# Transposes of q's and k's inputs, the squares of their angles, and the router's first rows moved to other places in one attention chunk's order

## The chip, the cores and the metric

The kernel runs on one NeuronCore of one Trainium2 chip. A core has five engines that run side by side, each with its own queue of instructions: TensorE (PE in the profile; its weight loads are PEld), VectorE (DVE), ScalarE (ACT), GpSimd (POOL) and SyncE (SP, which issues most DMA transfers here). Engines wait for each other through semaphores. The metric is the device time of one execution in microseconds (us). Before the change the median of three runs is 3440.44 us (3437.03 to 3441.25).

## What is computed

One pre-norm transformer block on x of shape (8, 1024, 512), in float32. Attention first, then a mixture of experts, each with its residual:

```python
theta_q = xh / (1.0 + jnp.abs(w_q)) + b_q + t * phi_q      # the same for k
sin_q, cos_q = lookup_sin_cos(theta_q)                     # table of 2048, linear interpolation
Q = jnp.concatenate([cos_q, sin_q], axis=-1)
V = cos_v + sin_v
scores = jnp.where(causal, -jnp.inf, jnp.einsum('bqhd,bkhd->bhqk', Q, K) / scale)
out = jnp.einsum('bhqk,bkhd->bqhd', jax.nn.softmax(scores, axis=-1), V).reshape(B, S, D)
theta_out = out / (1.0 + jnp.abs(w_out)) + b_out
...
x = x + attn(_layernorm(x))                                # 16 heads of 32
x = x + ffn(_layernorm(x))                                 # 8 experts, the best 2 of each token, 160 places each
```

The router of the experts takes a softmax over 8 logits of each token, keeps the best two, and numbers the tokens of each expert in order. The experts are two matrix products with a ReLU between.

## The kernel before

**Chunks.** Attention runs over 32 chunks, n = 0 to 31: batch b = n // 4, and c = n % 4 for the four heads (128 columns) that a chunk holds. A chunk has two pairs of heads. Each pair takes ten score tiles (`scores`, L591): matrix products into a PSUM tile of two banks, then one exponential on ScalarE (L620). `attend` (L626) multiplies the exponentials with v. `turn` (L658) transposes a pair's result back to tokens and divides by the sums. All score tiles, all transposes of `turn` and `qk_pre`, and all small products of the router take their PSUM tile from one pool, `ps_sc`, of three tiles in rotation: a new tile waits until the last reader of the tile three places before it is done.

**Sines.** For the next chunk's q and k, `qk_pre` (L479) transposes the normalized input (L202) and makes integer angles p on VectorE (L495, four instructions); `angle` (L425) shifts them left into r. ScalarE then takes two absolutes of r into c (L506), two squares of p's low half, in place (L430), and the sines of c and r (L514, L433). `qk_post` (L517) multiplies c and r with the squares on VectorE (L436) and sends each to the pairs' tiles with four transfers on SyncE's queue (L527). The pool `qkt` holds one buffer each of p, r and c: the shift into r for chunk n+2 may write only when the four transfers of r for chunk n+1 have read it. Sine and exponential are in different table sets of ScalarE, so that a chunk has two table loads; squares and absolutes need none. v (`v_pre`, `v_post`) and the attention's output (`o_pre`, `o_post`) go through the same steps: shift, sine, square, product.

**Residual and router.** `o_post` (L569) adds the output of chunk n-1 to x_mid (L575) and takes layernorm statistics of it (L577, eight instructions). When a batch's four chunks are in, `router` (L687) runs in steps that other code advances with `next(route)`: statistics to a mean and an inverse root, and the first two rows normalized (L704, by twos) and sent to DRAM (L710); then, four times, a feature step (L202 transposes of two rows, the copies L731 from PSUM to xT, the next two rows) and a sum step (L748 and L765 on TensorE, L770 and L772 on VectorE); then the choice of experts. Feature step g and sum step g belong together: L765 multiplies the xT that L731 wrote. `load_mid` (L370) loads the next batch's x into x_mid, on SyncE's queue, once the last two rows have been made from the old one.

**Order.** For TensorE, ScalarE and VectorE the order of instructions is the order in which the program emits them. The loop at L1202 writes it out with generators: `some(k, ...)` advances by k tiles, `rest` to the end. In the first half of chunk n (pair 0) it emits the last seven attend tiles of chunk n-1, in two pieces, each followed by five score tiles; `with_asides` sets small VectorE work between tiles. Then come `turn` of chunk n-1's second pair, `o_pre`, ten attend tiles of pair 0, the sines, and the first VectorE product of the next chunk. The second half (pair 1) emits two score tiles, `turn`, three score tiles, three attend tiles, five score tiles. Around these the code before has

```python
        if more:
            next_pairs = rest(post)
            v_post(n + 1, v_st)
        some(3, *ahead)
        router_step()
        if late:
            square(o_st[0])
            o_post(n - 1, o_st)
        some(3, attend(n, 1, 0, es[0], halves1))
        router_step()
        if late and c == 0:
            route = router(b - 1)
            next(route)
        some(5, *ahead)
        if n + 2 < NCK:
            qk_st = rest(qk_pre(n + 2))
            angle(*qk_st)
        if late and c == 0:
            next(route)
```

`late` is true from the second chunk on, `more` until the last but one, and `route` exists from n = 4 on. After the loop the expert half follows (L1134); the last batch's router runs in it (`ending`, L1331).

Of the kernel before, what the change touches and what calls it, by code (L numbers as in the profile page):

```python
# [73 lines left out]
def preln_attn_moe_kernel(  # L74
# [21 lines left out]
    nc = tc.nc  # L96
# [328 lines left out]
    def angle(p, r):  # L425
        nc.vector.tensor_scalar(r, p, TURN_SHIFT, None, ALU.logical_shift_left)

    def square(p):
        f = p.bitcast(U16).rearrange("p (s two) -> p s two", two=2)[:, :, 0]
        nc.scalar.activation(p.bitcast(F32), f, AF.Square, bias=split_c, scale=1.0 / FINE)  # L430

    def sine(r):
        nc.scalar.activation(r.bitcast(F32), r, AF.Sin, scale=STEP_ACT)  # L433
# [67 lines left out]
    def qk_abs(st):  # L501

        f, r = st
        c = qkt.tile([P, 2, S], F32, name="qk_c")
        for i in range(2):
            nc.scalar.activation(c[:, i, :], r[:, i, :], AF.Abs)  # L506
            yield c, f, r
        for i in range(2):
            square(f[:, i, :])
            yield c, f, r  # L510

    def qk_sin(st):
# [17 lines left out]
    def by_token(t):  # L530
        return t.rearrange("p (t f) -> p t f", f=P)
# [25 lines left out]
    def v_post(n, st):  # L557
        times(v_tiles[n % 2][:, :, :, :DH], heads(st[0]), heads(st[1].bitcast(F32)))


    def o_pre(n, pos):
        c = n % NCH
        p = pos.bitcast(I32)
        r = trig.tile([P, S], I32, name="t_r")
        nc.vector.tensor_tensor(by_token(p), by_token(pos), along(bias_o, c), ALU.add)
        angle(p, r)
        return p, r

    def o_post(n, st):  # L569
        f, s = st[0], st[1].bitcast(F32)  # L570
        b, ch = divmod(n, NCH)
        times(s, f, s)
        xt, stats = mid_tiles[b]
        xs = xt[:, :, ch * P : (ch + 1) * P]
        nc.vector.scalar_tensor_tensor(xs, by_token(s), SUM_UNIT, xs, ALU.mult, ALU.add)  # L575
        for t in range(NTT):
            nc.vector.bn_stats(stats[:, t, ch, :], xt[:, t, ch * P : (ch + 1) * P])  # L577

# [47 lines left out]
    def attend(n, pr, h, es, halves):  # L626

        vt = v_tiles[n % 2]
        av = ps_av.tile([P, 512], F32, name="av")
        tiles = tiles_of(h)  # L630
        for i, parts in enumerate(tiles):
            for kb, q0, w, at in parts:
                for a in range(2):
                    nc.tensor.matmul(  # L634
                        av[a * 64 : (a + 1) * 64, q0 - 512 * h :],
                        lhsT=vt[:, kb, 2 * pr + a, :], rhs=es[i][:, a, at : at + w],
                        start=kb == 0, stop=i + 1 == len(tiles),
                    )
            if i + 1 == len(tiles):
                av_sb = avp.tile([P, 512], F32, name="av_sb")  # L640
                q = 2 * (n % NCH) + pr
                nc.vector.tensor_scalar(av_sb, av, inv_o[:, q : q + 1], None, ALU.mult)
                halves.append(av_sb)
            yield

    def some(count, *gens):

        for gen in gens:
            while count and next(gen, 0) is None:
                count -= 1  # L650

    def rest(gen):
        got = None
        for got in gen:
            pass
        return got
# [214 lines left out]
    def keep(box, gen):  # L871
        for box[0] in gen:
            yield
# [311 lines left out]
    rest(base1)  # L1185
    mask()
    v_st = rest(v_pre(0))
    cs = qk_abs(qk_st)
    next(cs)
    qk_st = next(cs)  # L1190
    nc.scalar.activation(qk_st[0], qk_st[0], AF.Sin, bias=quarter_c, scale=-STEP_ACT)
    rest(cs)
    sine(qk_st[2])
    pairs = rest(qk_post(qk_st))
    sine(v_st[1])
    square(v_st[0])
# [2 lines left out]
    load_base(1)  # L1199
    last = None  # L1200
    o_st = route = first_rows = None
    for n in range(NCK):  # L1202
        more, late = n + 1 < NCK, last is not None
        b, c = divmod(n, NCH)
        if n == NCK - 1:
            to_inputs.close()
            first_rows = experts_begin()
        pos_n = trig.tile([P, S], F32, name="o_p")
        if late:
            e11, halves1, pos = last  # L1210
        es, halves = [[], []], [[], []]

        products = [attend(n, 0, h, es[h], halves[0]) for h in range(2)]
        if late:
            products.insert(0, attend(n - 1, 1, 1, e11, halves1))
        ahead = [scores(pairs[0], h, es[h]) for h in range(2)]
        places, v_box = [None], [None]
        absolutes = keep(places, qk_abs(qk_st)) if more else iter(())  # L1220
        asides = [keep(v_box, v_pre(n + 1))] if more else [first_rows]
        if b == 0 and c in (1, 2):
            asides.append(layernorm1(1, c - 1))
        elif c == 0 and b + 1 < B:
            asides.append(layernorm1(b + 1, 1))
        elif c == 3 and b + 2 < B:
            asides.append(layernorm1(b + 2, 0))

        router_step = lambda: next(route) if c == 1 and route is not None else None

        def with_asides(count):
            for _ in range(count):
                some(1, *ahead)
                for g in asides:
                    next(g, None)

        if late:
            some(3, *products)
        router_step()
        if c == 2 and route is not None:  # L1240
            next(route)
            asides.append(part(route))
        if n == 0:
            with_asides(3)
            qk_st = rest(qk_pre(1))
            angle(*qk_st)
            absolutes = keep(places, qk_abs(qk_st))
            with_asides(2)
        else:
            with_asides(5)  # L1250
        router_step()
        some(2, absolutes)
        if late:
            some(4, *products)
        router_step()
        with_asides(5)
        router_step()
        rest(absolutes)
        for g in asides:
            rest(g)  # L1260
        if more:
            v_st = v_box[0]
            square(v_st[0])
        if n == 1:
            load_mid(0)
        if late:
            turn(1, halves1, pos)
            o_st = o_pre(n - 1, pos)
        if c == 1 and b > 0:
            load_mid(b)  # L1270
        if n == 2:
            load_b1()
        if c == 2 and b + 2 < B:
            load_x(b + 2)
        if c == 3 and b > 0:
            next(route)
            if b > 1:
                fetch_slots(b - 2)
            scatter()


        some(3, *products)
        if more:
            qk_st = places[0]
            qk_sin(qk_st)
            sine(v_st[1])
        if late:
            sine(o_st[1])
        if more:
            post = qk_post(qk_st)  # L1290
            next(post)
        some(NTT, *products)
        if n == 0:
            load_base(2)


        es, halves1 = [[], []], []
        ahead = [scores(pairs[1], h, es[h]) for h in range(2)]
        router_step()
        if c == 2 and route is not None:  # L1300
            next(route)
        some(2, *ahead)
        turn(0, halves[0], pos_n)
        if more:
            next_pairs = rest(post)
            v_post(n + 1, v_st)
        some(3, *ahead)
        router_step()
        if late:
            square(o_st[0])  # L1310
            o_post(n - 1, o_st)
        some(3, attend(n, 1, 0, es[0], halves1))
        router_step()
        if late and c == 0:
            route = router(b - 1)
            next(route)
        some(5, *ahead)
        if n + 2 < NCK:
            qk_st = rest(qk_pre(n + 2))
            angle(*qk_st)  # L1320
        if late and c == 0:
            next(route)
        if n + 3 < NCK:
            load_base(n + 3)
        last = (es[1], halves1, pos_n)
        pairs = next_pairs if more else None
    rest(attend(NCK - 1, 1, 1, es[1], halves1))
    turn(1, halves1, pos_n)
    to_pairs.close()
# [1 line left out]
    def ending():  # L1331

        o_st = o_pre(NCK - 1, pos_n)
        yield
        sine(o_st[1])
        square(o_st[0])
        for _ in range(3):
            yield
        o_post(NCK - 1, o_st)
        for _ in range(3):  # L1340
            yield
        for name in router(B - 1):

            for _ in range(5 if name == "tiles" else 1):
                yield
        fetch_slots(B - 2)
        scatter()
        fetch_slots(B - 1)
# [33 lines left out]
```

## Time and profile before

| | us |
|---|---|
| median of three runs | 3440.44 |
| profiled execution, its own time | 3435.24 |
| its span, first to last instruction | 3433.3 |
| TensorE matmul busy | 3238.3 (94%) |
| VectorE busy | 2292.8 (67%) |
| ScalarE busy | 1319.5 (38%) |
| exponentials of the scores (L620), 640 | 566.5 busy, 938 ns each |
| score matmuls (L600), 3072 | 616.3 busy, 520 ns each |
| attend matmuls (L634), 3072 | 541.3 busy, 503 ns each |

Busy time is the union of an engine's instructions, and a share is that of the span. A row of the timeline gives the start, the time, the engine, the line, the operation with out<-in by the program's names, how many instructions were merged, and in brackets how long the engine sat idle before and what released it. A row of the waits gives who waited for whom: us in total, times, longest. Attention ends at about 1417 us; from there to the end the experts' matmuls run.

### The profile page before, as it was taken

What the parts mean: (1) busy time and instruction counts of PE and PEld (TensorE: products, weight loads), DVE (VectorE), ACT (ScalarE), POOL (GpSimd) and SP (SyncE); (2) the same over time, 40 slices, a digit from 0 to 9 for tenths busy, and PEclk for the clock granted to TensorE, in tenths of its full rate; (3) what the DMA queues carried; (4) which work ended last, traced back from release to release, by engine and by line L of the source; (5) the groups of instructions that cost most, each with busy time, mean ns of one, the idle gap of its engine ahead of it and who ended that gap; (6) DMA issues with size and microseconds to landing.
All of it is one profiled execution on the core that took longest, in us unless ns stands there. A gap on an engine that the chain in (4) does not pass through costs nothing.

```text
span 3433.3 us, 48857 instructions
## 1 busy us (share of the span) xinstructions
PE 3238.3 (94%) x18942; PEld 2176.1 (63%) x18942; DVE 2292.8 (67%) x5064; ACT 1319.5 (38%) x1609; POOL 411.8 (12%) x363
## 2 busy tenths in 40 slices
PE   3899998989898989999999999999999999999998
PEld 1444444444444444468878778778788688688687
DVE  7777777777777766565575566666656746745844
ACT  5786777777777777411111111111101101101201
POOL 1000202020202020331100100110111011011010
PEclk9999999999999999999999999999999999999999
DMA  5535353535353444232322412322322313322321
GB/s 145 143 88 160 93 155 97 151 100 148 106 166 106 116 111 124 75 92 65 110 57 54 111 50 62 108 47 65 107 43 71 104 39 79 102 43 82 97 40 25
DMA packets 233967, 320.79 MB, mean 93 GB/s; under 512 B 21528, under 2 KB 154376, under 8 KB 221320
## 3 DMA queue, kind: packets, MB, share of 16 engines
q1 hardware_dynamic: 211120, 275.47, 27.4%
q0 software_dynamic: 22528, 42.18, 6.9%
q8 instruction: 150, 2.46, 0.3%
q14 instruction: 81, 0.66, 0.1%
q10 hardware_dynamic: 88, 0.02, 0.0%
HBM read 188.67 MB, written 61.82 MB: 73 GB/s over the span
## 4 chain that ended last, share of the span: by engine, by line
PE 76%; ACT 14%; DVE 7%; DMA 1%; issue 1%; POOL 0%; POOLq 0%; SPq 0%; DVEq 0%; ACTq 0%
PE ps_p L1068 28%; PE ps_p L1023 25%; PE ps_s L600 12%; PE av L634 7%; ACT e L620 3%; ACT qk_f L430 2%; ACT qk_c L514 2%; ACT t_r L433 2%; ACT qk_r L433 2%; PE ps_s L202 1%; ACT L620 1%; ACT L514 1%; PE ps_t L979 1%; ACT v_p L430 1%; PE ps_s L614 1%
## 5 line engine op out<-in xcount | busy, mean ns | idle before, releaser
L600 PE MATMUL ps_s<-qk 64*128 64x512 f32 (+3 forms) x3072 | 616.3, 520 | 91.7 <-ACT e L620 61.6
L620 ACT ACTIVATE e<-ps_s 128x1024 f32<-128x1024 f32 (+1 forms) x640 | 566.5, 938 | 341.3 <-PE ps_s L614 186.2
L1068 PE MATMUL ps_p<-w,hid 128*128 128x256 f32 x2560 | 569.8, 380 | 0.0
L634 PE MATMUL av<-e,v 128*64 128x512 f32 (+3 forms) x3072 | 541.3, 503 | 0.0
L1068 PEld LDWEIGHTS ps_p<-w,hid 128*128 128x128 f32 x2560 | 484.7, 190 | 66.4
L600 PEld LDWEIGHTS ps_s<-qk 64*128 64x128 f32 x3072 | 264.5, 190 | 290.4 <-issue 143.6
L1068 PE MATMUL ps_p<-w_t,hid 128*128 128x256 f32 x1920 | 430.0, 379 | 0.0
L634 PEld LDWEIGHTS av<-e,v 128*64 128x64 f32 x3072 | 204.9, 140 | 317.0 <-issue 306.7
L1068 PEld LDWEIGHTS ps_p<-w_t,hid 128*128 128x128 f32 x1920 | 361.9, 190 | 47.7
L1023 PE MATMUL ps_p<-xe_s,t 128*128 128x256 f32 (+1 forms) x1024 | 299.2, 435 | 7.5 <-POOL t L1008 4.1
L1023 PE MATMUL ps_p<-xe,w 128*128 128x256 f32 (+1 forms) x1024 | 300.5, 437 | 1.5 <-DVE o_p L671 1.2
L1023 PE MATMUL ps_p<-xe,t 128*128 128x256 f32 (+1 forms) x1024 | 296.8, 433 | 0.0
L682 POOL DMA_INDIRECT slot_d<-token,slot x128 | 157.8, 1233 | 1107.7 <-issue 603.6
L1023 PEld LDWEIGHTS ps_p<-xe_s,t 128*128 128x128 f32 x1024 | 194.4, 191 | 92.6 <-DVE t L1008 7.9
L1097 ACT COPY p<-ps_p 128x256 f32<-128x256 f32 x40 | 14.8, 369 | 612.9 <-PE ps_p L1068 612.9
L1023 PEld LDWEIGHTS ps_p<-xe,w 128*128 128x128 f32 x1024 | 194.0, 191 | 84.5 <-DVE hid L1041 5.7
L1023 PEld LDWEIGHTS ps_p<-xe,t 128*128 128x128 f32 x1024 | 194.4, 190 | 80.9 <-issue 0.4
L1090 POOL DMA_INDIRECT out_dram<-y,slots x80 | 126.3, 1578 | 671.9 <-DVE y L1085 529.0
L962 POOL DMA_INDIRECT xg<-xn_d,source x80 | 78.3, 979 | 1052.5 <-PE ps_t L979 1015.9
L1038 ACT ACTIVATE p<-ps_p,b_t 128x256 f32<-128x256 f32 (+1 forms) x128 | 65.5, 511 | 329.7 <-DVE y L1084 169.7
L1042 ACT ACTIVATE hid<-hid 128x256 f32<-128x256 f32 (+1 forms) x128 | 60.1, 470 | 325.2 <-DVE hid L1041 325.2
L1055 ACT ACTIVATE hid<-hid,b_more 128x256 f32<-128x256 f32 (+1 forms) x128 | 71.9, 561 | 269.3 <-DVE hid L1054 269.3
(211 smaller groups left out, 3841.1 us busy)
## 6 DMA issues: line engine op xcount, KB each, us to landing
w<-in_L_ffn_W_dram SPq DMA_DIRECT2D x256, 256.0 KB
qk<-qk_c SPq DMA_DIRECT2D x128, 256.0 KB
qk<-qk_r SPq DMA_DIRECT2D x128, 256.0 KB
w<-in_L_ffn_W_dram SPq DMA_DIRECT2D x64, 512.0 KB
qk_base<-base_d SPq DMA_DIRECT2D x29, 1024.0 KB
xn_d<-xn SPq DMA_DIRECT2D x72, 256.0 KB
x_mid<-in_L_attn_x_dram SPq DMA_DIRECT2D x16, 1024.0 KB
out_dram<-x_mid SPq DMA_DIRECT2D x8, 2048.0 KB
```

The lines of the kernel that those rows point to most:

```text
L430: nc.scalar.activation(p.bitcast(F32), f, AF.Square, bias=split_c, scale=1.0 / FINE)
L433: nc.scalar.activation(r.bitcast(F32), r, AF.Sin, scale=STEP_ACT)
L514: nc.scalar.activation(c, c, AF.Sin, bias=quarter_c, scale=-STEP_ACT)
L600: nc.tensor.matmul(ps[:, a, at : at + w], lhsT=pair[r, 1, kb * P : (kb + 1) * P], rhs=pair[r, 0, q0 : q0 + w], start=at == 0, stop=not own ...
L620: nc.scalar.activation(e, ps[:, :, :n], AF.Exp, scale=UNIT * UNIT / math.sqrt(2 * DH))
L634: nc.tensor.matmul(av[a * 64 : (a + 1) * 64, q0 - 512 * h :], lhsT=vt[:, kb, 2 * pr + a, :], rhs=es[i][:, a, at : at + w], start=kb == 0, ...
L682: nc.gpsimd.indirect_dma_start(out=slot_d[b], out_offset=bass.IndirectOffsetOnAxis(ap=idx, axis=0), in_=src, in_offset=None,)
L962: nc.gpsimd.indirect_dma_start(out=xg, out_offset=None, in_=xn2_d[i % 2], in_offset=bass.IndirectOffsetOnAxis(ap=source[:, e, j0 + j, None ...
L1023: nc.tensor.matmul(ps, lhsT=weights[:, k, :], rhs=rows[:, k, :], start=k == 0, stop=k == 1)
L1055: nc.scalar.activation(h12, h12, AF.Relu, bias=more)
L1068: nc.tensor.matmul(ps, lhsT=hs[k][:, part, cols], rhs=ws[k][weight], start=k == 0, stop=k == NHQ - 1,)
L1090: nc.gpsimd.indirect_dma_start(out=out, out_offset=bass.IndirectOffsetOnAxis(ap=meta[:, e, jj[r], 0:1], axis=0), in_=ys[r], in_offset=None ...
```

## The change

No arithmetic changes; instructions move.

- `qk_abs` emits the two squares ahead of the two absolutes. In chunks with c other than 0, the squares of chunk n+2 are emitted at the end of chunk n, right behind the ten score tiles of its second pair, and the absolutes in the first half of chunk n+1, behind its fifth score tile. With c = 0 all four come there.
- The square of v moves ahead of the second piece of attend and the second five score tiles (it stood behind them).
- The transposes and angles of chunk n+2 (`qk_pre`) move from the end of the second half to a place behind the fifth score tile of pair 1, ahead of three attend tiles; with c = 0 they stay at the end.
- `o_post` becomes a generator: product and residual, then statistics. The square of o is emitted after the third score tile of pair 1 in place of the fifth. The shift of the angles stands between residual and statistics.
- With c = 0 the residual, its statistics and the router's beginning with the first two rows are emitted together, ahead of the three attend tiles; the first feature step moves into the next chunk. `v_post` moves behind these steps, with c = 0 to the end of the chunk.
- The router's steps in c = 1 and c = 2 are set with `route_on`: in c = 1 there are eight steps where there were seven, feature steps 0, 1 and 2 and sum steps 0 to 2 each at another place, feature step 3 behind the statistics, sum step 3 behind three attend tiles.

```diff
@@ def qk_abs(st):
         f, r = st
+        for i in range(2):
+            square(f[:, i, :])
+            yield
         c = qkt.tile([P, 2, S], F32, name="qk_c")
         for i in range(2):
             nc.scalar.activation(c[:, i, :], r[:, i, :], AF.Abs)
-            yield c, f, r
-        for i in range(2):
-            square(f[:, i, :])
             yield c, f, r
@@ def o_post(n, st):
         nc.vector.scalar_tensor_tensor(xs, by_token(s), SUM_UNIT, xs, ALU.mult, ALU.add)
+        yield
         for t in range(NTT):
             nc.vector.bn_stats(stats[:, t, ch, :], xt[:, t, ch * P : (ch + 1) * P])
@@ first half of a chunk
-        router_step = lambda: next(route) if c == 1 and route is not None else None
+        def route_on(slot):
+            if c == slot and route is not None:
+                next(route)
...
         if late:
             some(3, *products)
-        router_step()
+        route_on(1)
+        route_on(2)
         if c == 2 and route is not None:
-            next(route)
             asides.append(part(route))
...
             with_asides(5)
-        router_step()
-        some(2, absolutes)
-        if late:
-            some(4, *products)
-        router_step()
-        with_asides(5)
-        router_step()
-        rest(absolutes)
-        for g in asides:
-            rest(g)
+        route_on(1)
+        route_on(1)
+        rest(angles)
         if more:
             v_st = v_box[0]
             square(v_st[0])
+        if late:
+            some(4, *products)
+        route_on(1)
+        with_asides(5)
+        for g in asides:
+            rest(g)
         if n == 1:
             load_mid(0)
         if late:
             turn(1, halves1, pos)
             o_st = o_pre(n - 1, pos)
+        route_on(1)
         if c == 1 and b > 0:
             load_mid(b)
@@ second half of a chunk
-        router_step()
-        if c == 2 and route is not None:
-            next(route)
+        route_on(1)
+        route_on(2)
         some(2, *ahead)
         turn(0, halves[0], pos_n)
-        if more:
-            next_pairs = rest(post)
-            v_post(n + 1, v_st)
-        some(3, *ahead)
-        router_step()
+        next_pairs = rest(post) if more else None
+        some(1, *ahead)
         if late:
             square(o_st[0])
-            o_post(n - 1, o_st)
-        some(3, attend(n, 1, 0, es[0], halves1))
-        router_step()
-        if late and c == 0:
+            residual = o_post(n - 1, o_st)
+        some(2, *ahead)
+        begin = c == 0 and late
+        if begin:
+            rest(residual)
             route = router(b - 1)
             next(route)
+        elif n + 2 < NCK:
+            qk_st = rest(qk_pre(n + 2))
+        if late:
+            next(residual, None)
+        if n + 2 < NCK and not begin:
+            angle(*qk_st)
+        if late:
+            rest(residual)
+        route_on(1)
+        if more and not begin:
+            v_post(n + 1, v_st)
+        some(3, attend(n, 1, 0, es[0], halves1))
+        route_on(1)
         some(5, *ahead)
         if n + 2 < NCK:
-            qk_st = rest(qk_pre(n + 2))
-            angle(*qk_st)
-        if late and c == 0:
-            next(route)
+            if begin:
+                qk_st = rest(qk_pre(n + 2))
+                angle(*qk_st)
+            angles = keep(place, qk_abs(qk_st))
+            if not begin:
+                some(2, angles)
+        if more and begin:
+            v_post(n + 1, v_st)
         if n + 3 < NCK:
             load_base(n + 3)
```

Left out: the first chunk's own calls, which now take the four steps of `qk_abs` in their new order and the sines after them, and `ending`, which runs the new generator to its end in one go.

## The prediction

> **What bounds the kernel now.** I read the page's busy shares, then busy time by stretch, then TensorE's waits, then the timeline of one batch, engine by engine. The columns of the stretches: us, busy us of each engine with its count, TensorE clock granted, share of DMA, GB/s. The first four run from one chunk's first score tile of pair 1 (below: S1) to the next chunk's, for n=7, 8, 9, 10 (c=3, 0, 1, 2); the fifth is expert work.
>
> ```profile
> 371.06:409.72 38.66, 36.05 (x290) 17.49 (x289) 30.25 (x60) 31.87 (x33) 13.48 (x11) 1.00 0.34 83
> 409.72:461.42 51.70, 44.21 (x395) 21.47 (x393) 36.83 (x74) 33.62 (x34) 8.85 (x7) 0.90 0.58 178
> 461.42:501.64 40.22, 38.32 (x364) 18.90 (x360) 28.81 (x64) 30.88 (x33) 0.00 (x0) 1.00 0.49 140
> 501.64:541.59 39.95, 37.92 (x296) 17.80 (x289) 31.70 (x71) 31.63 (x33) 1.39 (x2) 0.96 0.32 80
> 1600.00:3420.00 1820.00, 1816.63 (x7764) 1447.06 (x7763) 1142.04 (x2694) 253.49 (x516) 181.81 (x141) 1.00 0.28 72
> ...
> PE ps_s L600 <- ACT e L620: 58.0, 38, 2.5
> PE ps_s L202 <- DVE xn L704: 30.1, 7, 4.7
> ...
> 415.00 0.70 PE L600 MATMUL ps_s<-qk 64*128 64x256 f32 x4 [2.49 <-ACT e L620]
> 415.54 0.25 PE L614 MATMUL ps_s<-later_b,keys_b 64*128 64x64 bf16 x4
> 415.92 3.68 PE L600 MATMUL ps_s<-qk 64*128 64x512 f32 x8
> ...
> 431.49 1.12 PE L202 MATMUL ps_s<-ident,xn 64*128 64x64 f32 x16 [4.62 <-DVE xn L704]
> ...
> 465.15 2.28 DVE L436 SCALAR_TENSOR_TENSOR qk_r<-qk_f,qk_r 128x2048 f32<-128x2048 f32 x1
> 467.35 1.22 DVE L436 SCALAR_TENSOR_TENSOR v<-v_p,t_r 128x1024 f32<-128x1024 f32 x1
> 468.57 1.29 DVE L731 COPY xT<-ps_s 128x512 f32<-128x512 f32 x2
> 470.23 1.23 DVE L436 SCALAR_TENSOR_TENSOR t_r<-o_p,t_r 128x1024 f32<-128x1024 f32 x1 [0.37 <-ACT o_p L430]
> ...
> 470.91 0.62 PE L765 MATMUL ps_s<-xT,wr_sb 128*32 128x256 f32 x8
> ```
>
> The expert half leaves TensorE 3 us idle in 1820: nothing to win there, and the change touches none of it. In the attention half TensorE is the bound too, but idles 2.61, 7.49, 1.90 and 2.03 us in the four stretches, 101 us over all 31 chunks, always for the same few releasers: the exponentials (58.0 us, 38 times) and the router's first rows (30.1 us, 7 times). The clock costs as well: the trace's clock record has it at half in 21 periods of 3.4 or 6.8 us between 166 and 1361 us, each just behind such an idle time. The matmuls of 415.92 take 3.68 us where the same eight take 1.99 at 466.05. A 3.4 us period costs about 1.65 us (the sine-to-sine time of a chunk is 38.66 us without one, 40.31 with).
>
> **The Trainium skill.** "TensorE: Matmul & The Clock Gate", HAM oscillation: idle times longer than the monitor's window bring the half clock, paid after the idle time. The trace agrees in the order of things, though idle times of 2.0 to 2.5 us, below the 3.4 us it gives, brought it too, in 14 of 22 cases. The same page, Architectural detail: VectorE and ScalarE take their instructions strictly in order, TensorE pulls only weight loads ahead. The trace shows no case against it (L765 starts after L748 throughout); so what stands ahead of L731 on VectorE holds up L765 and all scores behind it. "DMA: Bandwidth & Descriptors", Queues, rings and completion order: each DMA engine consumes one queue's descriptors in ring order. Landings agree: in n=9 the x_mid loads land at 462.8 (one of 16 shares at 465.4), the four qk_c from 465.0 to 468.3, the four qk_r at 470.4, 471.9, 473.2 and 474.1 (last share 475.0).
>
> **Part 1: squares moved (qk_abs, and square(v) ahead of the second five scores).** ScalarE's run before the second exponentials was 402.38 to 413.91 in n=8: three squares (3.24 us), table load, four sines, table load. Without the squares it starts at once after the last exponential and ends 3.2 us earlier, at S1+1.0; S1 itself takes 1.3 us, so its exponential ends at S1+2.65, when the turn's transposes (S1+2.8) end: the third tile waits no more. Gain: all of 2.49 (c=3 and c=0), 0.92 (c=1), 1.6 (c=2; with 0.3 of a turn that waited for the router's choice, whose work on VectorE comes after the cosine's product). The squares cost nothing where they land: 2.2 us of f after the tenth exponential, ahead of 3.4 to 3.6 us of idle; 1.14 us of v behind the absolutes, ahead of 1.16 to 2.44 us of idle. In c=0 all five (5.6 us) stand together, and delay the next exponentials 0.6 us, TensorE about 0.6. In the first chunk the cosine has the same work ahead of it either way: 0.
>
> **Part 2: q and k transposes earlier (0.66 us on TensorE, moved ahead of attend(n,1,0)).** The PSUM pool rotates over three tiles, and theirs comes free after the four L495 (2.73 us). S8 needs it 4 us later: covered. What is added on VectorE is order: qk_r product, L495, t_r, x_mid, the shift L426, statistics, v. L426 overwrites qk_r and so waits for the four qk_r transfers. They land 7.0 us after the product in c=3 (n=8: 415.73 to 422.75), a little sooner once qk_c goes earlier; L426 comes at 2.73+1.23+1.23, plus 0.9 for the transposes, 6.1 us after it. It waits about half a us, with only statistics, v and av_sb behind it: covered.
>
> **Part 3: residual, layernorm, first rows in one piece (c=0).** Without v and av_sb in between, and with o_p squared after three tiles, the chain is: product to 415.75, t_r and x_mid to 418.25, statistics 1.65, aggregates 1.1, inverse root 2.9, rows 1.25: 425.2, against 431.8. TensorE reaches the rows' transposes at 425.3 (S1 409.72, 2.13 two tiles, 0.6 turn, 2.83 three tiles, 2.31 attend, 4.37 five tiles, 0.6 transposes, 2.73 attend): the 4.62 us goes. But L495, L426 and v now stand behind the rows and ahead of L731: L495 ends 428.6, L731 432.3. The PSUM tiles that both read are in the ring of three, two and three places ahead of the next score tiles: of these the second, due at 426.95, waits for L495 until 428.65, and the third, due at 429.7, for L731 until 432.4: 4.4 us at the start of c=1. With the 0.6 of part 1, S1 of n=9 falls at 409.72 + 40.0 of work + 5.0 = 454.8; I add 1.3 for half clock: 46.4. Before, the stretch c=0 averages 50.7 (49.17 sine to sine in seven batches, plus 1.57 for the different start). Gain 4.3.
>
> **Part 4: the router's last copy in c=1, the large loss.** Before, L731 ran right after v at 468.57, and L765 found it ready at 470.91. After, feature step 3 stands behind L495, t_r, x_mid, L426 and eight statistics, while TensorE meets L765 behind one attend: at S1 + 2.13+0.6+2.83+0.6+0.6+2.31+0.15, 470.6. VectorE alone: product 467.43, transposes seen at 467.95, L495 to 470.7, t_r and x_mid to 473.2, L426 474.4, statistics 476.0, L731 477.3: a wait of 6.7. And L426 waits for qk_r: x_mid is loaded once the last two rows have been made, and these come behind turn and o_pre, L704 ending at 457.4 for 454.3. The queue is full from x_mid to qk_r, so all lands 3 us or less later: qk_r at about 476.4. L426 then ends at 477.7, statistics 479.3, L731 480.65. TensorE waits 10.1 us. Behind it the five score tiles, and ScalarE's exponentials, stand still. Less 1.77 of small waits that go (0.92, 0.33, 0.52) and 0.4 of smaller ones among the five tiles, plus 2.2 for half clock (n=8 after 4.62 us of idle: attend 4.73 us instead of 2.80, transposes 1.12 instead of 0.66): 10.1 lost.
>
> **Sum per batch.** c=3: 2.5 idle plus 0.6 x 1.65 clock, 3.5. c=2: 2.0 plus 1.0, 3.0. c=0: 4.3. c=1: -10.1. Together +0.7, seven times: 5 us. First batch: n=2 gives 3.9; n=0 and n=1 next to nothing, since the 6.6 us idle at 114.15 is VectorE behind two bases and a layernorm, which the change doesn't shorten. In all 9 us of the profiled execution's 3435.24 (span 3433.3, 1.9 around it). The median of the runs, 3440.44, lies 5.2 above it: 3431.
>
> Unknown costs, both ends: the qk_r landing in c=1 moves between 0 and 4.5 us (last share counted), so the wait is 6.7 to 11.5, or -24 to +10 us; half clock after it 0 to 3.4 us each, -15 to +8; half clock in the rest of attention gone altogether or as before, -8 to +15; the first two score tiles' stall in c=1 2 to 5.5 us, -17 to +8.
>
> **Rivals.**
> 1. The transfer doesn't matter: shares of qk_r land as before. For it, qk_c is issued earlier and the queue has a hole in n=9 (DMA share 0.79 and 0.69). Against it, x_mid fills 1.00 of 454.7 to 462.3 and moves later. Wait 6.7, 7 x 3.4 less: 3407.
> 2. The copy of xT isn't on the path, and all is gained: 7 x 10.1 more, 3360. Only if TensorE found other work; a matmul behind L765 cannot pass it. Little speaks for it.
> 3. Slower: qk_r waits for the slowest of 16 shares. In n=9 before one share of x_mid ran 2.5 us behind the rest. If that share meets x_mid, qk_c and qk_r in turn, L426 starts at 479.5 or later and the wait is 13 us; at 7 us per us of wait, break-even lies at 11.4. Time: 3431 + 7 x 3.2 = 3453. For it: the last qk_r of n=9 and of n=25 has a share 0.8 and 1.5 us behind the others. Against it: in the other chunks the shares mostly land within 0.2 us.
>
> **How the numbers follow.** Forecast 0.50 (own range 3415 to 3447), rival 1 0.14, rival 2 0.07, rival 3 0.29. The single likeliest time is 3431, 0.3% under the median, close to the 0.2% (7 us) that measurement can tell from no change. Of the forecast 0.29 lies under 3433.5, 0.18 within, 0.03 above; rivals 1 and 2 are faster; rival 3 gives 0.03 within, 0.26 above: 0.50, 0.21, 0.29. The range 3400 to 3462 leaves out rival 2 and the tails of 1 and 3.
>
> **What would show it.** Right: no wait of L600 for the exponentials over 1 us in c=0, 2, 3; L202 not waiting for L704; L600 waiting for L731 and L495 at the start of c=1; L765 waiting for L731 7 to 11 us seven times, and L426 for qk_r's landing before it. Wrong: L765 without a wait, which makes it 3360, or the half clock staying after every turn, which makes it slower.

## The result, and the profile after

The changed kernel takes 3409.9 us (median of five runs, 3403.52 to 3419.21), the kernel before 3438.55 in the same comparison: a ratio of 0.9917, 95% interval 0.9898 to 0.9935, so it is 0.8% faster. The profiled execution took 3403.52 us (span 3401.6), so 31.7 less than the profiled one of before; that difference is what the trace has to account for.

Busy time by stretch, cut at the same points (first score tile of pair 1; n=7, 8, 9, 10, which is c=3, 0, 1, 2) and once in the expert half:

```profile
364.15:400.03 35.88, 35.83 (x290) 17.58 (x288) 30.06 (x60) 32.03 (x33) 13.06 (x10) 1.00 0.36 90
400.03:443.44 43.41, 40.05 (x394) 20.18 (x392) 35.22 (x73) 33.06 (x33) 8.49 (x9) 1.00 0.63 184
443.44:494.74 51.30, 41.04 (x365) 19.95 (x361) 29.86 (x65) 31.50 (x33) 0.00 (x0) 0.87 0.46 137
494.74:530.61 35.87, 35.82 (x294) 17.56 (x288) 31.61 (x70) 31.66 (x33) 2.08 (x1) 1.00 0.32 83
1570.00:3388.00 1818.00, 1814.77 (x7755) 1446.97 (x7754) 1140.61 (x2688) 252.92 (x515) 180.61 (x141) 1.00 0.28 72
```

In c=3 and c=2 TensorE now idles 0.05 us, where it idled 2.61 and 2.03. c=0 is 8.29 us shorter than the stretch shown before, c=1 11.08 us longer. The expert half is as it was. TensorE's waits over the attention half (the releaser behind the arrow; us in total, times, longest):

```profile
PE ps_s L767 <- DVE xT L733: 74.8, 7, 12.3
PE ps_s L602 <- DVE xT L733: 11.8, 7, 1.7
PE ps_s L602 <- DVE qk_f L495: 10.3, 7, 1.5
```

The old list is gone: of the exponentials' 58.0 us in 38 waits one wait of 0.9 us is left, and L202 no longer waits for the rows of L704 (30.1 us, 7 times; L706 now). Instead one instruction waits seven times, 10.7 us each. L767 is L765 of before, L733 is L731, L602 is L600, L622 is L620. VectorE's timeline in c=1 of n=9 shows what L733 stands behind:

```profile
447.18 2.28 DVE L436 SCALAR_TENSOR_TENSOR qk_r<-qk_f,qk_r 128x2048 f32<-128x2048 f32 x1
449.56 2.73 DVE L495 SCALAR_TENSOR_TENSOR qk_f<-ps_s,inv_qk,qk_base 128x512 int32<-128x512 f32 x4
452.20 1.22 DVE L436 SCALAR_TENSOR_TENSOR t_r<-o_p,t_r 128x1024 f32<-128x1024 f32 x1
453.45 1.22 DVE L576 SCALAR_TENSOR_TENSOR x_mid<-t_r,x_mid 128x1024 f32<-128x1024 f32 x1
458.79 1.23 DVE L426 TENSOR_SCALAR qk_r<-qk_f 128x2048 int32<-128x2048 int32 x1 [4.11 <-DMA qk<-qk_r]
459.93 1.64 DVE L579 BATCH_NORM_STATS2 st_mid<-x_mid 128x6 f32<-128x128 f32 x8
461.48 1.27 DVE L733 COPY xT<-ps_s 128x512 f32<-128x512 f32 x2
```

The last number in brackets is idle time before the instruction and what ended it: of the 8.1 us between the end of x_mid (454.67) and the start of L767 (462.81, below), 4.11 are L426 waiting for the transfers out of qk_r. TensorE's timeline, at the start of c=1 and at L767:

```profile
418.53 1.14 PE L602 MATMUL ps_s<-qk 64*128 64x384 f32 x8 [1.46 <-DVE qk_f L495]
419.47 0.36 PE L616 MATMUL ps_s<-later_b,keys_b 64*128 64x128 bf16 x4
419.64 0.63 PE L602 MATMUL ps_s<-qk 64*128 64x256 f32 x4
420.07 0.28 PE L616 MATMUL ps_s<-later_b,keys_b 64*128 64x64 bf16 x4
422.04 1.55 PE L602 MATMUL ps_s<-qk 64*128 64x512 f32 x5 [1.68 <-DVE xT L733]
...
452.40 0.31 PE L750 MATMUL ps_s<-gather_e,lg 128*32 128x8 f32 x16
462.81 1.08 PE L767 MATMUL ps_s<-xT,wr_sb 128*32 128x256 f32 x8 [10.10 <-DVE xT L733]
463.82 5.42 PE L602 MATMUL ps_s<-qk 64*128 64x512 f32 x12
```

The twelve matmuls at 463.82 take 5.42 us. In the kernel before twelve of this form took 2.85 at full clock:

```profile
421.84 2.85 PE L600 MATMUL ps_s<-qk 64*128 64x512 f32 x12
```

So the half clock goes with the long wait. In the clock record its 21 periods of 3.4 or 6.8 us between 166 and 1361 us have become seven, of 10.2 to 13.7 us, one at each wait of L767: it begins inside the wait and outlasts it.

### The profile page after: what moved, and what is told of

It is laid out like the page before. It is cut to its first block, busy times and chain, and to the rows that moved or that the text cites. A ratio compares the mean times of both kernels' runs of the same rounds, so it can differ in the third digit from the quotient of the medians.

```text
span 3401.6 us, 48876 instructions
## 1 busy us (share of the span) xinstructions
PE 3205.5 (94%) x18942; PEld 2173.0 (64%) x18942; DVE 2285.9 (67%) x5064; ACT 1320.5 (39%) x1609; POOL 417.8 (12%) x363
## 4 chain that ended last, share of the span: by engine, by line
PE 57%; DVE 3%; DMA 1%; issue 1%; ACT 0%; POOL 0%; POOLq 0%; SPq 0%; DVEq 0%; ACTq 0%
PE ps_p L1070 28%; PE ps_p L1025 25%; PE av L636 1%; PE ps_s L602 1%; PE ps_t L981 1%; DMA slot_d<-token,slot 0%; DMA xn_d<-xn 0%; DMA out_dram<-y,slots 0%; DMA xg<-xn_d,source 0%; DMA qk<-qk_r 0%; DVE t L1010 0%; DVE t L1009 0%; ACT hid L1057 0%; DVE hid L1053 0%; DVE y L1086 0%
## 5 line engine op out<-in xcount | busy, mean ns | idle before, releaser
L622 ACT ACTIVATE e<-ps_s 128x1024 f32<-128x1024 f32 (+1 forms) x640 | 569.3, 937 | 299.2 <-PE ps_s L602 202.8
L602 PE MATMUL ps_s<-qk 64*128 64x512 f32 (+3 forms) x3072 | 605.7, 513 | 55.4 <-DMA qk<-qk_r 21.4
L636 PE MATMUL av<-e,v 128*64 128x512 f32 (+3 forms) x3072 | 524.4, 491 | 0.0
L602 PEld LDWEIGHTS ps_s<-qk 64*128 64x128 f32 x3072 | 267.2, 191 | 246.9 <-issue 154.6
## 6 DMA issues: line engine op xcount, KB each, us to landing
x_mid<-in_L_attn_x_dram SPq DMA_DIRECT2D x16, 1024.0 KB, 10.1
```

What stands on the lines that cost most here:

```text
L602: nc.tensor.matmul(ps[:, a, at : at + w], lhsT=pair[r, 1, kb * P : (kb + 1) * P], rhs=pair[r, 0, q0 : q0 + w], start=at == 0, stop=not own ...
L622: nc.scalar.activation(e, ps[:, :, :n], AF.Exp, scale=UNIT * UNIT / math.sqrt(2 * DH))
L636: nc.tensor.matmul(av[a * 64 : (a + 1) * 64, q0 - 512 * h :], lhsT=vt[:, kb, 2 * pr + a, :], rhs=es[i][:, a, at : at + w], start=kb == 0, ...
```

## The experiments

Labels are those of the runs; each is compared with the kernel before, run on the same chip. Line numbers are the changed kernel's unless said otherwise. Stretches given below are means over seven batches, from a chunk's first score tile of pair 0 to the next chunk's. The table above cuts half a chunk later, so that the stall at the start of c=1 counts to c=0 there and to c=1 here; for c=3 it makes no difference, for c=2 at most 0.4 us.

### e1_copy_first: the last feature copy ahead of the residual

```diff
+        route_on(1)
         if late:
             next(residual, None)
         if n + 2 < NCK and not begin:
             angle(*qk_st)
         if late:
             rest(residual)
-        route_on(1)
```

> The changed kernel, with the last feature copy of c=1 (L733) issued right behind the q and k transposes, ahead of t_r, x_mid, the shift L426 and the statistics; nothing else moves. Theory (order on VectorE holds L767 up): L733 is done 1.3 us after L495, the wait of L767 falls from 10.7 us to about 1.2, and the half clock of 10 to 14 us behind it goes; 10 to 11 us in each of seven batches, 3410 - 74 = 3336 (3325 to 3345). Rival (the late landing of qk_r is the bound and comes back elsewhere): L426 still waits 3 to 4 us, now with v, av_sb and the next q and k behind it, TensorE waits 5 us at another place: 3370 to 3380. Second rival (TensorE is limited by ScalarE's exponentials behind, so that a wait only moves): 3395 to 3410.

Measured: 3346.09 us, ratio 0.9738 (0.9721 to 0.9756). TensorE's waits:

```profile
PE ps_s L750 <- DVE prob L774: 14.1, 7, 3.1
PE ps_s L602 <- DVE xT L733: 11.8, 7, 1.7
PE ps_s L602 <- DVE qk_f L495: 10.2, 7, 1.5
PE ps_s L767 <- DVE xT L733: 5.8, 7, 0.8
```

L767's wait fell from 74.8 us to 5.8, and of the seven long half clock periods two of 3.4 us were left. So the order on VectorE held L767 up. But some 10 us of the expected gain are missing, and the first rival has a part in that: L426 still waits for qk_r's landing (2.83 us in n=9), and behind it now stand the statistics, v, av_sb, and then L772 and L774 of the router's last-but-one sum step. L750 waits for these, 1.3 to 3.1 us.

### e2_shift_behind_copy: only the shift moved

```diff
         if late:
             next(residual, None)
-        if n + 2 < NCK and not begin:
-            angle(*qk_st)
         if late:
             rest(residual)
         route_on(1)
+        if n + 2 < NCK and not begin:
+            angle(*qk_st)
```

> The changed kernel, with only the shift L426 of the early q and k moved behind the last feature copy of c=1; t_r, x_mid and the eight statistics stay ahead of it. It measures the share of qk_r's landing in the wait of L767. Theory: x_mid ends at 454.65 in n=9, the statistics 456.3, L733 457.6; the wait of L767 is 5 to 5.5 us instead of 10.7, 5.2 us a batch less and perhaps 1 of clock: 3410 - 36 to 43 = 3367 to 3374. Rival (the landing is not what holds L426 up, only its place counts): 1.2 us a batch less, 3400.

Measured: 3368.87 us, ratio 0.9807 (0.9787 to 0.9827), as the theory had it. VectorE in n=9:

```profile
450.00 1.27 DVE L733 COPY xT<-ps_s 128x512 f32<-128x512 f32 x2
452.70 1.23 DVE L426 TENSOR_SCALAR qk_r<-qk_f 128x2048 int32<-128x2048 int32 x1 [1.44 <-DMA qk<-qk_r]
```

TensorE there:

```profile
451.32 1.08 PE L767 MATMUL ps_s<-xT,wr_sb 128*32 128x256 f32 x8 [4.89 <-DVE xT L733]
```

Of the 10.1 us in n=9, 5.2 are the shift: 4.1 of waiting for the transfer and about 1.2 of its own. The other 4.9 are t_r, x_mid, the statistics and the copy itself.

### e3_squares_only: part 1 alone, on the kernel before

```diff
-        some(2, absolutes)
-        if late:
-            some(4, *products)
+        rest(angles)
+        if more:
+            v_st = v_box[0]
+            square(v_st[0])
+        if late:
+            some(4, *products)
         router_step()
         with_asides(5)
         router_step()
-        rest(absolutes)
...
-        if more:
-            v_st = v_box[0]
-            square(v_st[0])
```

> The kernel before, with the squares of q, k and v moved alone: squares and absolutes behind the first five scores, square(v) there too; q and k transposes, residual and rows stay where they were. Theory: the waits for the exponentials (58.0 us, 38 times) go without a successor, and the half clock behind them too: c=3 3.5, c=2 3.0, c=0 2.5, c=1 0.9 a batch, and 4 in the first: 3438 - 73 = 3365 (3355 to 3375). It would mean that the other two parts together cost 45 us in the changed kernel. Rival (the third tile's exponential then waits for something else, squares that now stand behind the tenth exponential delay the next ones): 3395 to 3425.

Measured: 3396.93 us, ratio 0.9872 (0.9849 to 0.9895), within the rival's range. Part 1 alone thus gains at least as much as the whole change (0.9917, and 0.9895 when measured again below). The waits for the exponentials fell from 58.0 us to 29.2, over 36 times; the half clock behind them is gone from the clock record, and seven periods at the waits for the rows stay. One of TensorE's lines of n=8, with the line numbers of the kernel before:

```profile
391.21 1.14 PE L600 MATMUL ps_s<-qk 64*128 64x384 f32 x8 [1.11 <-ACT e L620]
```

ScalarE ahead of it:

```profile
385.13 2.00 ACT L506 ACTIVATE qk_c<-qk_r 128x1024 f32<-128x1024 int32 x2
387.02 2.18 ACT L430 ACTIVATE qk_f<-qk_f,split_c 128x1024 f32<-128x1024 uint16 x2
389.10 1.14 ACT L430 ACTIVATE v_p<-v_p,split_c 128x1024 f32<-128x1024 uint16 x1
390.14 4.24 ACT L620 ACTIVATE e<-ps_s 128x1024 f32<-128x1024 f32 x5
```

Five operations in one block, 5.0 us from 385.13 to 390.14, stand ahead of the second five exponentials, and the attend tiles beside them last 3.2 us. The fourth of the five score tiles behind them then waits 1.1 us. c=3 came to 37.43 us instead of 35.88 in the changed kernel (39.84 before). There the squares of q and k have a second place, at the end of the chunk before.

### e4_rows_as_before: part 3 undone

```diff
         begin = c == 0 and late
         if begin:
+            v_post(n + 1, v_st)
             rest(residual)
-            route = router(b - 1)
-            next(route)
...
+        if begin:
+            route = router(b - 1)
+            next(route)
         some(5, *ahead)
...
                 angle(*qk_st)
+                next(route)
```

(Behind the first five score tiles one `route_on(1)` goes as well, and so does the later `v_post` of c=0.)

> The changed kernel, with c=0 and the start of c=1 in the order of the kernel before (v ahead of the residual, rows behind the attend, the router's first feature step at the end of c=0); squares and the early q and k of the other chunks stay. It measures part 3 alone. Theory: the wait of L202 for the rows returns (4 to 4.7 us, and 1.3 to 1.7 of half clock), the two waits of L602 at the start of c=1 (3.15 us) go; c=0 3 to 5 us longer in each of seven batches: 3410 + 21 to 34 = 3431 to 3444, with L767 waiting about 10 us as before. Rival (one wait for another, no half clock): 3405 to 3418.

Measured: 3436.81 us, ratio 0.9998 (0.9988 to 1.0008). TensorE's waits:

```profile
PE ps_s L767 <- DVE xT L733: 75.4, 13, 11.7
PE ps_s L202 <- DVE xn L706: 27.3, 7, 4.0
```

The wait for the rows is back, 3.9 us each, and with it one half clock period of 3.4 us or more in each batch. Beside the other parts, part 3 is worth 27 us, its own two new waits at the start of c=1 deducted. Without it, the gain of the squares and the loss at L767 cancel to nothing.

### e5_qk_late: part 2 undone

```diff
-        elif n + 2 < NCK:
-            qk_st = rest(qk_pre(n + 2))
         if late:
             next(residual, None)
-        if n + 2 < NCK and not begin:
-            angle(*qk_st)
...
         if n + 2 < NCK:
-            if begin:
-                qk_st = rest(qk_pre(n + 2))
-                angle(*qk_st)
+            qk_st = rest(qk_pre(n + 2))
+            angle(*qk_st)
             angles = keep(place, qk_abs(qk_st))
```

> The changed kernel without part 2: q and k transposes, L495 and the shift L426 go back behind the last five score tiles in every chunk; the squares of f follow them at the end of the chunk, the rest as in the changed kernel. Theory (part 2 put L495 and the waiting L426 ahead of L733, and hides squares): in c=1 the product ends at 449.5, t_r and x_mid 452.0, statistics 453.6, L733 454.9, TensorE meets L767 0.6 us sooner, at 451.9: it waits 3 us instead of 10.7 and little half clock is left, 8 to 10 us a batch less; in c=2 and c=3 the two squares (2.2 us) now stand ahead of the first exponential of the next pair and bring about 1 us of wait each: 3410 - 7 x 9 + 7 x 2 = 3361 (3350 to 3375). Rival (the wait of L767 comes from the residual and statistics, part 3, not from part 2): L767 still waits 8 us or more, 3400 to 3415.

Measured: 3397.64 us, ratio 0.9866 (0.9849 to 0.9882). TensorE's waits:

```profile
PE ps_s L602 <- ACT e L622: 35.7, 22, 1.7
PE ps_s L767 <- DVE xT L733: 22.2, 8, 3.9
```

The time is neither the theory's nor the rival's. What concerns L767 came as the theory had it: about 3 us instead of 10.7, so part 2, not part 3, made most of that wait. The cost of the squares was set too low. At the chunk's end they now come after the late L495 and L426 and ahead of the next pair's first exponential. TensorE waits 1.5 to 1.7 us for it, and three stretches of four (c=3, 0 and 2) take 37.88, 38.63 and 37.93 us for 35.88, 36.43 and 36.17; expected was 1 us in two. So the early q and k earn about 6.0 us a batch for the squares and lose 8.1 in c=1: beside the other two, part 2 made the kernel no faster.

### e6_copy_first_shift_last

```diff
+        route_on(1)
         if late:
-            next(residual, None)
-        if n + 2 < NCK and not begin:
-            angle(*qk_st)
-        if late:
             rest(residual)
-        route_on(1)
...
         some(3, attend(n, 1, 0, es[0], halves1))
         route_on(1)
+        if n + 2 < NCK and not begin:
+            angle(*qk_st)
```

> The changed kernel, with the copy L733 ahead of the residual as in the copy-first run, and the shift L426 behind the router's sum step, after attend and L772. Theory (in the copy-first run L426 still waits 2.8 us for qk_r, and L772 behind it makes L750 wait 1.3 to 3.1 us, with two half clock periods in seven batches): L750's waits go, L767 keeps 0.8; 2.0 us of idle and about 0.5 of clock a batch less than 3346: 3328 (3323 to 3334). Rival (L426 later makes the absolutes or another step late): 3346 or more.

Measured: 3359.66 us, ratio 0.9753 (0.9735 to 0.977): not faster than e1, the rival. The intervals of the two ratios overlap, but in the profiled executions the four stretches together take 1.5 us a batch longer than in e1. ScalarE at the end of n=7 (c=3):

```profile
372.29 2.19 ACT L430 ACTIVATE qk_f<-qk_f,split_c 128x1024 f32<-128x1024 uint16 x2 [2.11 <-DVE qk_r L426]
374.39 1.91 ACT L622 ACTIVATE e<-ps_s 128x1024 f32<-128x1024 f32 x2
```

TensorE just behind it, and in c=1 of n=9:

```profile
375.44 1.13 PE L602 MATMUL ps_s<-qk 64*128 64x512 f32 x4 [0.88 <-ACT e L622]
...
453.97 0.70 PE L602 MATMUL ps_s<-qk 64*128 64x256 f32 x4 [1.09 <-DVE prob L774]
```

The squares write over qk_f, which the shift must have read first. In c=2 and c=3 a late shift makes them late, they hold up the next exponential, and two stretches of four (c=3 and c=0, 37.00 and 37.94 us) are 1.1 and 1.5 us longer than in e1. L750's waits did go, but the tenth score tile of c=1 now waits 1.09 us for L774.

### e7_and_v_shift_late: e6, and the shift and v of c=0 behind the first feature copies

```diff
         route_on(1)
+        for f in held:
+            f()
+        held = []
...
                 qk_st = rest(qk_pre(n + 2))
-                angle(*qk_st)
+                held = [lambda s=qk_st: angle(*s), lambda n=n, s=v_st: v_post(n + 1, s)]
...
-        if more and begin:
-            v_post(n + 1, v_st)
```

> The copy-first, shift-last kernel, in which also the shift L426 and v of c=0 wait until the first feature copies of c=1 (L733) are issued. Theory: L733 comes right behind L495, 2.3 to 2.4 us sooner; the wait of the third score tile of c=1 for L733 (1.68 us) falls to 0.1 or none, the one for L495 (1.46) stays: 1.6 us in each of seven batches, 11 less than the run without it: 3317 (3311 to 3324). Rival (the waits for L495 and L733 are one chain, and what goes from the second comes back at the next router step): no more than 3 us less.

Measured: 3368.72 us, ratio 0.9786 (0.9769 to 0.9804), 9 us slower than e6 on the same chip: the rival, and worse. TensorE's waits:

```profile
PE ps_s L602 <- DVE qk_f L495: 11.9, 7, 1.8
PE ps_s L767 <- DVE xT L733: 11.4, 14, 0.8
PE ps_s L750 <- DVE lg L772: 10.3, 5, 2.6
```

The wait of L602 for L733 (11.8 us) did go, and it came back at L750 and L767, the next router steps. Shift and v, 2.4 us, now stand between L706 and L772. But they are not all that does: in n=9 L706, right ahead of them, waits for a transfer of rows to DRAM.

```profile
413.84 1.00 DVE L706 TENSOR_SCALAR xn<-x_mid,mv,rstd 128x512 f32<-128x512 f32 x2 [1.75 <-DMA xn_d<-xn]
```

Waits of L706 for such transfers come to 0.8 to 3.4 us in six of the seven batches; in e6 there is one, of 0.5 us. So the run does not show that VectorE has no room there: whether shift and v between L733 and L706 would have been covered, no run tried.

### e8_copy_first_shift_after_v, and the changed kernel again

```diff
+        route_on(1)
         if late:
-            next(residual, None)
-        if n + 2 < NCK and not begin:
-            angle(*qk_st)
-        if late:
             rest(residual)
-        route_on(1)
         if more and not begin:
             v_post(n + 1, v_st)
+        if n + 2 < NCK and not begin:
+            angle(*qk_st)
```

> The copy-first kernel, with the statistics and v of every chunk other than c=0 ahead of the shift L426 instead of behind it. The shift-last run lost 0.92 us in c=2 and c=3 each because the squares overwrite qk_f and so wait for L426; here L426 ends at 453.5 on the time axis of the copy-first run (n=9), before the first square at 453.75. Theory (the landing wait of L426 is covered by the statistics and v): L426 waits 0 to 1.5 us, L772 comes 2.1 us sooner, L750's waits (14.1 us) go, c=2 and c=3 stay at 36.24 and 35.88: 3346 - 12 to 18 = 3328 to 3334. Rival (the tenth score tile takes the sum step's PSUM tile, as in the shift-last run, and waits for L774 1 to 2.6 us): 3340 to 3352.

> The changed kernel as it is, on the same chip, for comparison: 3410 (3403 to 3419), whatever theory holds.

Measured: 3338.7 us, ratio 0.9708 (0.9691 to 0.9725); the changed kernel on the same chip 3404.94, ratio 0.9895 (0.9878 to 0.9911). L426 waits 0.74 us for the landing in n=9, and L750 no longer waits. The time lies between the two expectations: c=3 and c=0 did not stay, but grew by 0.47 us each. TensorE's line of n=7:

```profile
334.38 2.04 PE L602 MATMUL ps_s<-qk 64*128 64x512 f32 x8 [0.21 <-ACT e L622]
```

It is e6's effect, smaller: in c=2 and c=3 L426 ends 1.0 us later in the chunk than in the changed kernel (in e6 1.7 us later), and the first square starts 0.03 or 0.04 us behind it in all three kernels.

### e10_shift_after_v_in_c1: the late shift in c=1 alone

```diff
+        route_on(1)
         if late:
             next(residual, None)
-        if n + 2 < NCK and not begin:
+        if n + 2 < NCK and not begin and c != 1:
             angle(*qk_st)
         if late:
             rest(residual)
-        route_on(1)
         if more and not begin:
             v_post(n + 1, v_st)
+        if n + 2 < NCK and c == 1:
+            angle(*qk_st)
```

> The kernel of the last run but one, with the shift L426 behind the statistics and v only in c=1; in c=2 and c=3 it stands ahead of them, as in the changed kernel. Theory (in that run the squares of f waited for L426 in c=2 and c=3, and the third score tile of the next pair for them, 0.21 us, 0.47 us a stretch): the stretches of c=3 and c=0 return from 36.35 and 36.90 to 35.88 and 36.43, c=1 stays at 46.8: 3338.7 - 6.6 = 3332 (3329 to 3336). Rival (the 0.47 us come from something else in that order): 3338.

Measured: 3330.2 us, ratio 0.969 (0.9672 to 0.9708), as expected; c=3, c=0 and c=1 are 35.88, 36.43 and 46.74 us. The ratio alone does not part it from e8, the stretches do. It has the lowest ratio of this study: it is 3.1% under the kernel before, where the changed one is 0.8 and 1.1% under it in two comparisons. By these ratios it is 70 to 78 us faster than the changed kernel. TensorE's waits that are left in the attention half:

```profile
PE ps_s L602 <- DVE xT L733: 11.8, 7, 1.7
PE ps_s L602 <- DVE qk_f L495: 10.1, 7, 1.5
PE ps_s L767 <- DVE xT L733: 5.8, 7, 0.8
```

No half clock period is left between 118 and 1312 us.

## Why the prediction was right, and where its sizes were off

The direction held, and so did the waits that were named: those for the exponentials and the rows went, two smaller ones came at the start of c=1, and L767 waits for L733 behind qk_r's landing, seven times, 9.8 to 12.3 us (two of the seven are longer than the 11 it named). The size did not: the gain was 28.7 us by the medians, three times the 9 that were forecast, and the time, 21 us under the forecast, lies outside the forecast's own range of 3415 to 3447. It is near the time of rival 1, but not for its reason, and that is chance: in rival 1 qk_r lands as early as before and the wait is 6.7 us, and it is 10.7.

**c=1, the loss.** The forecast set L767 at S1 + 9.2, L426's end at S1 + 16.3, L733's end at S1 + 19.2. In n=9 after the change they are at S1 + 9.3, 16.6 and 19.3, and the wait 10.10 for the forecast 10.1; the mean of seven is 10.7. The half clock behind it costs 2.7 us of busy time (41.04 for 38.32 before), forecast 2.2. e1 and e2 show that the cause is the order on VectorE, and that half of it is the shift, most of that its waiting for qk_r's landing. That the later x_mid load makes this landing late is read from the queue and not shown by a run that moves the load alone: in n=9 the four qk_r are issued from 449.49 on and the last lands at 458.76, 9.3 us; in n=7, with no x_mid load, 6.8 us. One rival can be looked at: part 2 also moves the load of qk_base ahead, to 9.4 us behind S1 in n=9, where it was at 19.2. In e5 it is issued at S1 + 21.4 and qk_r still lands late: in c=1 15.2 us behind S1 in the mean of seven, against 13.1 before and 15.8 after the change. That leaves 0.6 us of the 2.7 for the load of qk_base.

**Rival 3** named a real effect: in n=9 nine of the 16 shares of the last qk_r transfer have landed by 457.30, fifteen by 458.05, the last one lands at 458.76, and L426 starts at 458.79. The one late share costs 0.7 us there (in all four qk_r transfers it comes 0.7 to 0.9 us behind the others), and the longest wait of the profile is 12.3. But the mean, 10.7, stays under its break-even of 11.4. In e9, the same kernel profiled again, the mean is 10.9 and the longest 14.6.

**c=3 and c=2.** Forecast 3.5 and 3.0 us; the stretches, whose means hold the half clock, went from 39.84 to 35.87 and from 39.59 to 36.17, 4.0 and 3.4, since the half clock left altogether. What the forecast had wrong here is which part earns it: it gave all to the squares. e3 has 1.1 us a chunk coming back at the next exponentials, and e5 1.5 to 1.7, so squares and early q and k earn it together. Part 2 put L426's wait in these chunks at half a us; it is 1.6 to 2.3, and nothing on TensorE waits behind it, as forecast. The line "in c=0 all five stand together" priced that block at 0.6 us; in the changed kernel, where router steps stand beside it, TensorE waits for none of it.

**c=0, the step that was mis-sized.** The forecast made the stretch 46.4: 40.0 of work, a stall of 4.4 at the start of c=1, 0.6 for the squares, 1.3 of half clock. In n=8 it took 43.4: 40.05 busy and 3.14 of stall, no 0.6, no half clock. Three us seven times are 21 us, of which c=1, 0.8 us longer than forecast, takes back 5. The two waits exist and have the releasers that were named; L202's wait for the rows is gone. But the forecast put the second wait on the third score tile, by strict rotation of the three PSUM tiles. In the trace the third tile starts at 419.64, before L733, and the fourth waits for L733: one more tile of work lies under the wait, which is 1.68 instead of 2.7.

```profile
420.70 1.28 DVE L733 COPY xT<-ps_s 128x512 f32<-128x512 f32 x2
```

And two idle times of 1.46 and 1.68 us, with 1.8 us of matmuls between, brought no half clock in any of seven batches, where e4's single one of 3.8 to 4.0 us brought it in all seven.

**The sum.** In the profiled executions: c=3 and c=2 7.4 us less a batch, c=0 and c=1 together 3.6 more (90.60 to 94.19), 3.8 seven times, 26.6; the chunks before n=3 3.5 less (forecast 3.9), the end 1.6 less: 31.7. The forecast had 0.7 a batch. Of the 3.1 between, 2.2 is c=0 and c=1 and 0.9 is c=3 and c=2.

Seen by kind of time, the gain is not less waiting. Over the seven batches, from the first score tile of n=3 to that of n=31, TensorE is idle 97.3 us before and 100.2 after (101.7 in e9), and busy 1092.9 and 1063.4. The clock record has half clock for 88.7 us of that in both, and the mean granted clock of the two profiles is the same, 0.982. But before, 77.5 us of it fell on matmuls, and after only 32.5: the rest passes while TensorE waits at L767. At half clock the twelve matmuls above take 1.9 times as long, so an estimate from the 45 us of half clock work that went is 21 to 23 us, most of the 26.6. The forecast's own terms for half clock come to some 1.6 us a batch (1.0 in c=3, 1.0 in c=2, about 1.8 in c=0, less 2.2 in c=1), where TensorE's busy time fell by 4.2: that is most of what it missed.

## What to carry to other kernels

A step that is moved earlier on an in-order engine puts all its instructions ahead of those that kept their place, and its waits too: list what is now behind each instruction that can wait for a transfer, and ask who waits for that. Here 75 us of new waits at L767 and 22 at the start of c=1 took the place of the 88 that went, and moving one pair of copies, with the shift behind v in one chunk of four, won 70 to 78 us more than the change itself. An operation that overwrites its input ties the place of its other reader as well: because the squares work in place, a later shift cost time in c=2 and c=3. In c=1 it cost next to nothing: in e10 the stretch behind it, c=2, takes 36.20 us for 36.17.

## What the runs showed of the hardware that was not expected

The length of an idle time does not by itself tell whether half clock follows. Waits of 3.8 to 4.7 us for the rows brought it 21 times out of 21 (before, e3, e4). In the kernel before, idle times of 2.0 to 2.5 us brought it in ten of 15 cases and those of 1.6 us in four of seven; the prediction counts these 22 together and calls them 2.0 to 2.5 us. In e5, 21 idle times of 1.5 to 1.7 us brought none. In e1 it came after waits of L750 of 2.83 and 2.47 us, and not after one of 3.06. What decides between such cases these runs do not show.

Nor does it always come behind the idle time, as the prediction has it: at all seven waits for the rows of the kernel before it begins inside the wait. So it does at L767: in n=9 of the changed kernel TensorE is idle from 452.7, the record shows half clock from 455.4, and it lasts 13.65 us, some 6.2 us beyond the end of the wait. Over the seven waits it begins 2.0 to 3.5 us after TensorE falls idle and ends 3.2 to 6.2 us after the wait does.

The PSUM tiles of the pool were not reused in strict rotation, which concerns the program's choice of tiles more than the chip. Beside the start of c=1: in e6 the tenth score tile of pair 1 waits for L774 and L750 does not; in e1 the tenth runs before L774, and L750 waits for it. Moving a VectorE instruction by a few places changed who waited for the tile of the sum step.
